# A two-convolution residual layer by lookup on one core: the first two blocks' patch sets as double sets of six transfers, with the transfer queue's order and one image's statistics moved

## The chip, the cores and the metric

The kernel runs on one of the eight cores of a Trainium2 chip. A core has TensorE (PE in the profile: the matrix array; PEld is its weight load), VectorE (DVE), ScalarE (ACT), GpSimd (POOL) and SyncE (SP, which in this kernel only starts transfers). Each engine takes its instructions in the order in which they were written and waits for others by semaphores. Transfers between the chip's main memory (DRAM) and the core's on-chip memory (SBUF) run on 16 DMA engines beside the compute engines; PE writes its results into PSUM banks, which other engines read out.

The metric is the device time of one execution in microseconds (us). Shown are the median of several executions and one execution taken by the profiler.

## The reference

Input `x` is 16 images of 256 channels of 28 x 28, float32. The layer is

```python
h   = gn(x)                        # group norm, 32 groups of 8 channels
out = relu(bn1(amm(h, centroids1, wsub1)))
out = bn2(amm(out, centroids2, wsub2))
out = out * sigmoid(relu(mean(out) @ w1 + b1) @ w2 + b2)     # per channel
y   = x + relu(out + h)
```

`amm` stands for a 3 x 3 convolution done approximately: for each channel the 9 values under the window (the patch, zero padded) are compared with 16 centroids of that channel, and the sum over all channels of a softmax-weighted lookup is the output:

```python
d    = sum(p * p) - 2 * p . centroid + sum(centroid * centroid)
attn = softmax(-d over the 16 centroids)
out  = sum over channels and centroids of attn * (centroid @ wsub)
```

The kernel uses that the sum over centroids of attn times centroid is a soft-selected patch of nine values per channel (numerators over a weight sum), which is then multiplied with `wsub` as an ordinary matrix product over 9 x 256 values.

## The kernel before, in words

**Tiling.** Two convolutions (l = 0, 1) times 16 images times four blocks make 128 blocks. A block is half of the channels (`hh`, 128 of 256) on half of the image rows (`t`, 14 of 28, N = 392 positions); the four blocks of an image go in the order (hh, t) = (0,0), (0,1), (1,1), (1,0). Images are numbered from 0, and so are blocks.

**One block.** (1) `patches` (L395) reads the nine shifted copies of the padded rows of 128 channels from a padded image in DRAM (`home1`, `home2`) into two SBUF tiles, p = 0 and 1, each of 8 slots with 8 channels per slot: six transfers per tile (the list `PIECES`), so twelve per block. A transfer writes every 8th partition (16 partitions) or, for three of the six, every 16th (8 partitions). One row of the tile per channel is a constant 1, written once at the start. (2) `logits` (L409) multiplies the patches with the centroids: four groups `mm` = 0 to 3 of 16 products; mm 0 and 1 read tile p = 0, mm 2 and 3 tile p = 1. Results `lg` lie in PSUM. (3) `exps` (L420, ACT) writes e = exp(2 lg), two instructions per group. (4) `num_b` (L474) forms the weight sums `nb` from the four e; ACT and DVE put them together (L484, L488, L494, L499), DVE takes the reciprocal (L502) and spreads it over partitions (`spread`, L517, two shuffles per group). (5) `num_a` (L460) forms the numerators `na` from e; three groups are read out by DVE with the reciprocal multiplied in (`scale_a`, L536), the others copied by ACT (`copy_a`, L530) and multiplied by POOL (`scale_q`, L525). The results are the tiles `qp` (pairs) and `qo`. (6) `product` (L544) multiplies nine such tiles with a weight matrix into `acc`. The products of the four blocks are combined as in a Strassen scheme of seven products, one of them issued in two parts: weights A11, A12, A22 and the sums S1 to S4, made by `combine` (L226), and differences of the q tiles, made by `mix` on POOL (L553).

**The start.** The weights and image 0 are loaded, `norm0` takes the group norm of image 0 for each channel half (`gn_stats` L339/L340 on DVE, the mean over groups by two small products on PE, L345 and L362, their read-outs on DVE, L349 to L364, the inverse root on POOL, L276 to L368, and `gn_apply` L374 on ACT into a padded tile `xpad`), and `to_home1` (L386) writes that tile to DRAM, where the patches come from. `center_wd` prepares the centroid weights.

**Where the tiles lie.** `pts` are the two ordinary patch tiles. Block 1 reads its patches into `alts`, which are the not yet filled weight tiles `walls` (two tiles of three weight matrices), so that it need not wait for block 0 to be done with `pts`. The twelve pair tiles `qp0` to `qp11` are separate tiles.

**Order.** There is no scheduler at work: `at(cl, sub, f, ...)` files every step under a key (clock, sub), and at the end all are issued in the order of the keys. So the key alone sets where a step stands on each engine's queue. A block takes two clocks. SP's order at the start is: the two halves of channel half 0 to `home1`; twelve patch transfers of block 0; channel half 1 to `home1` (key -0.95); twelve of block 1 (-0.9 and -0.4); six of block 2's first tile (0, 1.5); weight A11 (0, 1.55); image 1 (0, 1.65); six of block 2's second tile; weights S3 and A22; block 3; and so on. Issues that depend on a landing, or on a buffer's last reader, hold up everything behind them on SP.

**Statistics of the next image.** Image 1's `gn_stats` has key (3, 1.3), its two small products (4, 0.81) and (4, 0.83), in the midst of the first product, which is cut into three parts (0.8, 0.82, 0.84) of 4, 2 and 3 weight slices around them. Image 2's load has (6, 2.6) and its `gn_stats` (8, 0.3).

## Time and profile before

| what | value |
|---|---|
| median of 3 executions | 2630.59 us (2630.03 to 2636.79) |
| the profiled execution | 2632.19 us, of which the profile's span is 2630.7 us |
| PE busy | 2587.2 us, 98% of the span |
| VectorE, ScalarE, GpSimd busy | 1766.0, 1360.6, 1902.8 us (67%, 52%, 72%) |
| DMA | 374.37 MB in 217831 packets, mean 142 GB/s |

The profile is of one execution. Times in it are counted from the start of the span. A row of the timeline gives start, length, engine, line, operation, what it writes and reads, how many instructions are merged in it, and in brackets the engine's idle time before it with what ended that. [...] Rows of engine "SPq" are the issues of transfers: their length is the time of issuing, not of the transfer. In the chain of work that ended last a row "DMA a<-b" runs from a transfer's issue to its landing. "PEclk" is the share of TensorE's full clock that was granted.

### The profile page before, as it was taken

To read this page: it belongs to the slowest core of one execution; us is meant where nothing else is said; L and a number is where in the kernel's file an instruction comes from. 1 tells how busy PE (TensorE), PEld (TensorE's weight loads), DVE (VectorE), ACT (ScalarE), POOL (GpSimd) and SP (SyncE) were. 2 spreads that over 40 slices of the span, in tenths; PEclk is the share of its full clock that TensorE was granted. 3 is DMA by queue.
4 is the path that set the end of the run, shared out by engine and by line. 5 is a ranking of instruction groups with operands and counts; after the bars stand their busy time and mean duration, and the time that the engine had idled before them with its cause. 6 is when DMAs were issued, how large, how long until landed. Compare 5 with 4: busy or idle time off the path is not lost.

```text
span 2630.7 us, 85667 instructions
## 1 busy us (share of the span) xinstructions
PE 2587.2 (98%) x36984; PEld 1267.9 (48%) x36984; DVE 1766.0 (67%) x3759; ACT 1360.6 (52%) x1876; POOL 1902.8 (72%) x1320
## 2 busy tenths in 40 slices
PE   6999999999999999999999999999999999999997
PEld 2444454444544445444444444444444444444444
DVE  5776566666567665666666776767776667767665
ACT  4444444445444444444454555555555655555653
POOL 3876667766667766677667777778878787777786
PEclk9999999999999999999999999999999999999999
DMA  8656655665455566655664444444444444444441
GB/s 209 163 154 180 186 162 162 189 182 165 140 147 146 175 184 173 173 151 154 169 168 107 111 116 117 127 115 117 106 126 128 118 118 110 117 119 125 114 121 47
DMA packets 217831, 374.37 MB, mean 142 GB/s; under 512 B 29752, under 2 KB 188008, under 8 KB 217448
## 3 DMA queue, kind: packets, MB, share of 16 engines
q1 hardware_dynamic: 211272, 336.16, 47.8%
q0 software_dynamic: 6176, 32.66, 3.4%
q8 instruction: 295, 4.83, 0.8%
q14 instruction: 88, 0.72, 0.1%
HBM read 288.93 MB, written 79.80 MB: 140 GB/s over the span
## 4 chain that ended last, share of the span: by engine, by line
PE 96%; DMA 2%; DVE 1%; POOL 0%; ACT 0%; SPq 0%; issue 0%; DVEq 0%; POOLq 0%; ACTq 0%
PE acc L544 52%; PE lg L409 17%; PE na L460 14%; PE nb L474 13%; DMA xt<-in_x 1%; DMA wall<-home 1%; DMA pt<-home 0%; PE sep L846 0%; DVE gn_st L339 0%; DVE rb L517 0%; SPq L395 0%; DMA home<-xpad 0%; POOL qp L553 0%; PE sep L835 0%; PE gnp L362 0%
## 5 line engine op out<-in xcount | busy, mean ns | idle before, releaser
L544 PE MATMUL acc<-qp,wall 128*128 128x392 f32 x3072 | 1096.8, 500 | 1.7 <-POOL qp L553 0.9
L420 ACT ACTIVATE e<-lg 128x784 f32<-128x784 f32 x960 | 738.0, 821 | 638.2 <-PE lg L409 635.1
L553 POOL TENSOR_TENSOR qp<-qp,qp 128x784 f32<-128x784 f32 x512 | 944.9, 1869 | 158.6 <-DVE qp L536 158.1
L544 PEld LDWEIGHTS acc<-qp,wall 128*128 128x128 f32 x3072 | 565.2, 190 | 509.1 <-issue 55.3
L517 DVE STREAM_SHUFFLE rb<-r 128x392 f32<-128x392 f32 x1024 | 551.0, 605 | 0.0
L409 PE MATMUL lg<-pt,wd 32*32 32x392 f32 x16256 | 483.4, 502 | 7.3 <-DMA pt<-home 2.7
L488 DVE SCALAR_TENSOR_TENSOR r<-nb,kst,r 128x392 f32<-128x392 f32 x128 | 80.0, 625 | 452.6 <-ACT r L484 438.8
L536 DVE TENSOR_TENSOR qp<-na,rb 128x784 f32<-128x784 f32 x351 | 333.0, 972 | 64.7 <-PE na L460 53.7
L460 PE MATMUL na<-e,cwa 64*32 64x392 f32 x8192 | 374.8, 492 | 0.7 <-DVE hpad L581 0.7
L474 PE MATMUL nb<-e,cwb 64*32 64x392 f32 x8192 | 374.8, 493 | 0.1
L525 POOL TENSOR_TENSOR qo<-qo,rb 128x392 f32<-128x392 f32 x128 | 131.3, 1026 | 314.1 <-DVE rb L513 313.6
L502 DVE RECIPROCAL r<-r 128x392 f32<-128x392 f32 x128 | 333.2, 2603 | 4.4
L525 POOL TENSOR_TENSOR qp<-qp,rb 128x784 f32<-128x784 f32 x161 | 297.9, 1860 | 2.9
L474 PEld LDWEIGHTS nb<-e,cwb 64*32 64x32 f32 x8192 | 192.4, 107 | 174.3 <-issue 19.5
L460 PEld LDWEIGHTS na<-e,cwa 64*32 64x32 f32 x8192 | 182.9, 106 | 183.5 <-issue 76.2
L409 PEld LDWEIGHTS lg<-pt,wd 32*32 32x32 f32 x16256 | 121.2, 103 | 283.1 <-issue 252.1
L544 PE MATMUL acc<-qp,w_A 128*128 128x392 f32 x512 | 183.9, 502 | 0.0
L484 ACT ACTIVATE r<-nb,kst 128x392 f32<-128x392 f32 x128 | 86.7, 677 | 164.0 <-PE nb L474 164.0
L444 POOL TENSOR_TENSOR z<-z,mx 128x1568 f32<-128x1568 f32 x32 | 91.8, 2869 | 94.7 <-DVE mx L438 94.7
L544 PE MATMUL acc<-qo,wall 128*128 128x392 f32 x384 | 157.7, 492 | 0.0
L530 ACT COPY qp<-na 128x784 f32<-128x784 f32 x161 | 130.8, 812 | 27.0 <-PE na L460 25.2
L544 PEld LDWEIGHTS acc<-qp,w_A 128*128 128x128 f32 x512 | 95.0, 191 | 83.0 <-DVE qp L536 19.8
(154 smaller groups left out, 1646.8 us busy)
## 6 DMA issues: line engine op xcount, KB each, us to landing
pt<-home SPq DMA_DIRECT2D x762, 209.0 KB
pt<-home SPq DMA_DIRECT2D x762, 104.5 KB
home<-xpad SPq DMA_DIRECT2D x31, 899.0 KB
xt<-in_x SPq DMA_DIRECT2D x30, 784.0 KB
out_dram<-y SPq DMA_DIRECT2D x32, 392.0 KB
d_wS<-st SPq DMA_DIRECT2D x12, 192.0 KB
wall<-d_wS SPq DMA_DIRECT2D x4, 576.0 KB
wall<-in_ws SPq DMA_DIRECT2D x3, 576.0 KB
```

What stands on the lines that cost most here:

```text
L409: nc.tensor.matmul(bk[32 * c : 32 * c + 32, :N].rearrange("p (r w) -> p r w", w=W), lhsT=wts["wd", u["hh"]][32 * i : 32 * i + 32, mm, c, : ...
L420: nc.scalar.activation(eg[:, 2 * i : 2 * i + 2, :], bk[:, :, :N], AF.Exp, scale=2.0)
L444: nc.gpsimd.tensor_tensor(zk, zk, mx.unsqueeze(2).to_broadcast([P, N // 4, K]), ALU.subtract)
L460: nc.tensor.matmul(bs[32 * i : 32 * i + 32, r, :N], lhsT=wts["cwa", u["hh"]][64 * r : 64 * r + 64, mm, i, :], rhs=es[64 * r : 64 * r + 64, ...
L474: nc.tensor.matmul(bs[32 * i : 32 * i + 32, r, :N], lhsT=wts["cwb", u["hh"]][64 * r : 64 * r + 64, mm, i, :], rhs=es[64 * r : 64 * r + 64, ...
L502: nc.vector.reciprocal(u["r"], u["r"])
L517: nc.vector.stream_shuffle(rb[:, r, :], u["r"], mask_of(2 * mm + r))
L525: nc.gpsimd.tensor_tensor(q, q, u.pop(("rb", mm)), ALU.mult)
L530: nc.scalar.copy(pair(u, mm), u.pop(("na", mm))[:, :, :N])
L536: nc.vector.tensor_mul(pair(u, mm), u.pop(("na", mm))[:, :, :N], rb)
L544: nc.tensor.matmul(accs[key][:, :N], lhsT=wl[w][:, k, :], rhs=us["q", k], start=first and n == 0, stop=last and n == len(ks) - 1,)
L553: nc.gpsimd.tensor_tensor(pair(out_u, mm), pair(in0, mm), pair(in1, mm), ALU.subtract)
```

## The change

Blocks 0 and 1 get both of their patch tiles as one double set: six transfers of 16 slots instead of twelve of 8. Block 0's lies in the space of the pair tiles qp0 to qp8, which become one tile `qwall`; block 1's in the weights, which become one tile `wall`. Six setups of ones (four before) are filled at the start, POOL's two, ACT's four. On SP, channel half 1 goes to `home1` after block 1's set, and weight A11 ahead of block 2's first tile. Three of block 1's `spread` steps (six shuffles) move from before image 1's read-outs on DVE to between and behind them, and the first product is cut as 5, 2 and 2. Image 2's load goes behind block 4's second tile, and its `gn_stats` one clock later; image 1's channel half 1 goes to `home1` behind that load.

```diff
-    walls = [wpool.tile([P, 3, NS, P], F32, name=f"wall{i}") for i in range(NPT)]
-    wl = {n: walls[i // 3][:, i % 3] for i, n in enumerate(("S1", "S2", "S4", "A12", "S3", "A22"))}
+    wall = wpool.tile([P, 6, NS, P], F32, name="wall")
+    wl = {n: wall[:, i] for i, n in enumerate(("S1", "S2", "S4", "A12", "S3", "A22"))}
...
-    alts = [
-        w.rearrange("p a s n -> p (a s n)")[:, : 8 * PTW].rearrange("p (s n) -> p s n", n=PTW) for w in walls
-    ]
+    qwall = const.tile([P, 9, 2, N], F32, name="qwall")
+    both = [
+        t.rearrange("p a b n -> p (a b n)")[:, : 16 * PTW].rearrange("p (s n) -> p s n", n=PTW) for t in (qwall, wall)
+    ]
...
-        "pair": [const.tile([P, 2, N], F32, name=f"qp{i}") for i in range(NQ["pair"])],
+        "pair": [qwall[:, i] if i < 9 else const.tile([P, 2, N], F32, name=f"qp{i}") for i in range(NQ["pair"])],
...
+    def patches_both(u):
+        at0 = u["hh"] * P * 2 * HROW + RT * u["t"] * PW
+        n = PTW - 2
+        for dy, dx in PIECES:
+            step = 16 if dx else 8
+            o = both[u["r"]][TAPS[dy][dx] :: step, :, :n]
+            rows, slots = [step // 8 * HROW, P // step], [16 * HROW, 16]
+            nc.sync.dma_start(o, view(home1[0], at0 + dy * PW + dx, [rows, slots, [1, n]]))
...
-            u["pt", p] = alts[p] if j == 1 else pts[p]
-            if j == 1:
-                at(-0.4 if p else -0.9, 0.0, patches, u, p)
+            u["pt", p] = both[j][:, 8 * p : 8 * p + 8] if j < 2 else pts[p]
+            if j < 2:
+                if p == 0:
+                    at(*((-0.9, 0.0) if j else (-2, 1.5)), patches_both, u)
...
-                at(g - 1, 2.05 if i == 4 - len(kept) and j > 1 else 1.4 + 0.01 * i, spread, u, mm)
+                if j == 1:
+                    at(4, 0.835 if i else 0.815, spread, u, mm)
+                else:
+                    at(g - 1, 2.05 if i == 4 - len(kept) and j > 1 else 1.4 + 0.01 * i, spread, u, mm)
...
-                    for sub, k0, k1 in ((0.8, 0, 4), (0.82, 4, 6), (0.84, 6, 9)):
+                    for sub, k0, k1 in ((0.8, 0, 5), (0.82, 5, 7), (0.84, 7, 9)):
...
-                    at(*((g - 2, 2.6) if b else (0, 1.65)), load_x, b + 1)
+                    at(*((g - 2 + (b == 1), 2.6 - (b == 1)) if b else (0, 1.65)), load_x, b + 1)
...
-                        at(*((g, 0.3) if b else (3, 1.3)), gn_stats, b + 1, q)
+                        at(*((g + (b == 1), 0.3) if b else (3, 1.3)), gn_stats, b + 1, q)
...
-                        at(*((g + 4, 1.92) if b else (4 + 2 * q, 1.6)), to_home1, b + 1, q)
+                        at(*((g + 4, 1.92) if b else (4 + 3 * q, 1.6 + 0.05 * q)), to_home1, b + 1, q)
...
-    at(0, 1.55, load_w, 0, "A11")
+    at(0, 1.45, load_w, 0, "A11")
...
-    nc.scalar.activation(pts[0].rearrange("p s n -> p (s n)"), one.to_broadcast([P, 8 * PTW]), AF.Copy)
+    ones(both[0][:, :8], "act")
     norm0(0)
     for i in range(2):
         to_home1(0, 0, i)
-    nc.gpsimd.memset(pts[1], 1.0)
-    nc.gpsimd.memset(alts[0], 1.0)
-    nc.scalar.activation(alts[1].rearrange("p s n -> p (s n)"), one.to_broadcast([P, 8 * PTW]), AF.Copy)
+    ones(both[0][:, 8:], "pool")
+    ones(both[1][:, :8], "act")
+    ones(both[1][:, 8:], "pool")
+    for t in pts:
+        ones(t, "act")
...
-    at(-0.95, 0.7, to_home1, 0, 1)
+    at(-0.7, 0.7, to_home1, 0, 1)
```

`ones(t, eng)` fills a tile with 1.0, by an ACT activation or by a POOL memset.

More of the change, by code (lines that the diff above doesn't have):

```diff
@@ L1134, in center_wd, with ones @@
         center(wts["wd", hh].rearrange("p a b c -> p (a b c)"), 512)
-    nc.scalar.activation(pts[0].rearrange("p s n -> p (s n)"), one.to_broadcast([P, 8 * PTW]), AF.Copy)
+    def ones(t, eng):
+        t = t.rearrange("p s n -> p (s n)")
+        if eng == "act":
+            nc.scalar.activation(t, one.to_broadcast([P, 8 * PTW]), AF.Copy)
+        else:
+            nc.gpsimd.memset(t, 1.0)
+    ones(both[0][:, :8], "act")
     norm0(0)
```

## The prediction

> **What bounds the kernel now.** First the page: which engine is full, what the last chain consists of, and the size of the larger patch transfers.
>
> ```profile
> span 2630.7 us, 85667 instructions
> PE 2587.2 (98%) x36984; PEld 1267.9 (48%) x36984; DVE 1766.0 (67%) x3759; ACT 1360.6 (52%) x1876; POOL 1902.8 (72%) x1320
> PE 96%; DMA 2%; DVE 1%; POOL 0%; ACT 0%; SPq 0%; issue 0%; DVEq 0%; POOLq 0%; ACTq 0%
> ...
> pt<-home SPq DMA_DIRECT2D x762, 209.0 KB
> ```
>
> PE is the bound. It lacks 2630.7 - 2587.2 = 43.5 us, and all the change can touch is in there, or in slow records. Where it lies is told by the busy time by stretches (columns: stretch, its length, then busy us and instructions of PE, PEld, DVE, ACT, POOL, then granted clock, DMA share, GB/s).
>
> ```profile
> 0.00:20.00 20.00, 5.48 (x14) 3.51 (x14) 10.14 (x23) 8.22 (x4) 11.62 (x23) 1.00 0.74 217
> 40.00:60.00 20.00, 16.27 (x287) 6.61 (x271) 16.35 (x47) 10.54 (x15) 4.71 (x3) 1.00 0.98 216
> 120.00:140.00 20.00, 20.00 (x291) 10.02 (x290) 15.77 (x41) 10.32 (x15) 7.02 (x8) 1.00 0.32 82
> 2600.00:2631.00 31.00, 18.04 (x64) 10.28 (x62) 11.31 (x18) 11.49 (x21) 16.84 (x11) 0.83 0.14 55
> ```
>
> From 120 us on PE is full until the tail; 14.5 us are idle in the first stretch, 13.0 in the last, which isn't touched, and nearly all the rest between 20 and 120. So the change can win only what PE loses in there. PE's timeline shows the losses one by one:
>
> ```profile
> 23.64 3.21 PE L409 MATMUL lg<-pt,wd 32*32 32x392 f32 x64 [1.07 <-DVE wd L309]
> 29.07 2.63 PE L409 MATMUL lg<-pt,wd 32*32 32x392 f32 x64 [2.23 <-DMA pt<-home]
> 37.65 2.75 PE L409 MATMUL lg<-wall,wd 32*32 32x392 f32 x64 [2.30 <-DMA wall<-home]
> 49.25 2.07 PE L409 MATMUL lg<-pt,wd 32*32 32x392 f32 x48 [0.47 <-DMA pt<-home]
> 52.31 2.90 PE L544 MATMUL acc<-qp,w_A 128*128 128x392 f32 x8
> 56.47 0.39 PE L345 MATMUL gnp<-gn_mv,gmat 128*128 128x4 f32 x2 [1.26 <-DVE gn_mv L340]
> 59.95 0.38 PE L362 MATMUL gnp<-gn_dv,gmat 128*128 128x2 f32 x2 [1.67 <-DVE gn_dv L353]
> 61.11 2.82 PE L544 MATMUL acc<-qp,w_A 128*128 128x392 f32 x4
> 99.48 0.95 PE L409 MATMUL lg<-pt,wd 32*32 32x392 f32 x32 [1.99 <-DVE qo L499]
> 101.94 2.21 PE L460 MATMUL na<-e,cwa 64*32 64x392 f32 x48 [0.66 <-DVE hpad L581]
> ```
>
> Until 50 us PE waits for patches; around 56 to 60 for image 1's statistics; at 99.5 for DVE, which was late for another reason, shown below.
>
> **The change, part by part.** *The double sets.* Bytes and rows are the same; twelve issues become six. SP's issues, and the chain's transfers:
>
> ```profile
> 14.54 7.59 SPq L395 DMA_DIRECT2D pt<-home  x12
> 22.55 0.58 SPq L386 DMA_DIRECT2D home<-xpad  x1
> 23.40 12.08 SPq L395 DMA_DIRECT2D wall<-home  x12
> ```
>
> ```profile
> 10.37 4.15 DMA home<-xpad
> 19.66 6.55 DMA pt<-home
> 26.23 8.65 DMA wall<-home
> 34.89 7.98 DMA wall<-home
> 42.94 11.03 DMA xt<-in_x
> 54.00 1.05 DVE gn_st L339 x2
> 56.36 3.05 DVE rb L517 x6
> 80.36 12.99 DMA xt<-in_x
> ```
>
> Issues pause for landings (26.23 starts where the transfer of 19.66 lands, 34.89 where that of 26.23 does, 42.94 where that of 34.89 does), and the time to landing grows from 4 to 8 and 11 us: transfers queue up, and issuing (0.6 us each) is not the pace. What a single-tile set costs alone is seen where nothing else moves; the digits are the busy tenths of the DMA engines in 40 slices of 104 to 114 us, 0.25 us each:
>
> ```profile
> DMA  0000000200658965987989866444553100000000
> DMA packets 650, 0.99 MB, mean 99 GB/s; under 512 B 72, under 2 KB 648, under 8 KB 648
> ```
>
> 22 busy slices (the 11th to the 32nd), 5.5 us for 0.96 MB of patches: 11 us per block.
>
> Block 0: logits now start at 23.64 on half the set, and at 29.07 on the other half. All six long transfers span both tiles, so no logit can start before all land: between 23.64 and 29.07, near the upper end since the bytes are the same. I take 28.3: 0.8 less, because the write of channel half 1 (22.55) no longer mixes in. That is 4.7 us later than now for the first logits. What hid work there was ACT, whose exps of the first half ran before the second half was there; only the last four stand after it:
>
> ```profile
> 30.05 3.07 ACT L420 ACTIVATE e<-lg 128x784 f32<-128x784 f32 x4 [1.70 <-PE lg L409]
> 35.49 0.68 ACT L484 ACTIVATE r<-nb,kst 128x392 f32<-128x392 f32 x1 [2.37 <-PE nb L474]
> ```
>
> Afterwards all eight come in a row: 28.3 + 0.98 (30.05 - 29.07) + 2 x 3.07 + 2.37 = 37.8 for the sums' read-out, 2.3 late against 35.49. It costs only if block 1's patches aren't later still.
>
> Block 1: now its first tile is there at 37.65 and its second at 42.87 (34.89 + 7.98). Afterwards both together, 11 us of transfers after 28.3: 39.3. Bounds 37.65 and 42.87. So block 1's first logits start 39.3 - 37.65 = 1.65 later (0 to 5.2), and what hangs on them (its sums, then its reciprocal and image 1's statistics on DVE, then the first statistics product on PE) comes 1.65 later too: 56.47 + 1.65 = 58.1. Image 1's load (42.94 + 11.03 = 53.97) is just in time now.
>
> *The write of channel half 1* goes behind block 1's set, and block 2's first transfers read what it writes. It lands at 39.3 + at most 4.15, then 7.0 us for a set (104.0 plus 32 slices less its issue at about 105): 50.5. PE wants it at 49.25 - 0.47 + 1.65 = 50.4: no cost, but no slack. Behind that wait on SP stand image 1's load, block 2's second tile, S3 and A22, and go with it. The load's 0.8 MB take 4.6 us at a set's pace: 55.1, wanted at 54.00 + 1.65 = 55.65; what it is later than that counts in full. Weight A11, moved ahead of it, is used at 52.31; it costs nothing where it moves while SP waits for that write.
>
> *Six shuffles and the cut of the product.* The six (3.05 us at 56.36) stand before the read-out of the first product; that is the 1.67 wait at 59.95. Afterwards they stand behind. After 58.1: 0.39 for the product, then 0.54 for the read-outs on DVE (59.41 to 59.95), meanwhile PE does 4 records (2.90 / 8 each, 1.45): second product at 59.95, ending at 60.35, 4 more records, 61.8. In the trace `acc` ends at 61.11 + 2.82 = 63.93. Gain 2.1 us (3.75 if block 1 is not later, -1.45 at 5.2). Late next: two shuffles (0.51 each) stand before `gn_var` and four behind; the last ends at about 62.6, and the numerators that want them come at 61.8 + 0.95 (logits) + 0.74 (a third of 2.21) = 63.5.
>
> *Setups of ones.* ACT gets two more, before the second channel half's apply:
>
> ```profile
> 10.24 2.99 ACT L1142 ACTIVATE wall<-one 128x3360 f32<-128x3360 f32 x1
> 20.59 1.04 ACT L374 ACTIVATE xpad<-xt,nrm 128x784 f32<-128x784 f32 x1 [7.36 <-POOL nrm L368]
> ```
>
> 2 x 2.99 = 5.98 fit into the 7.36 us in which ACT waits for POOL: nothing; 1.4 us more and that write would be late, which goes last anyway. POOL's two stand where its two were.
>
> *Image 2.* Its load, issued at 80.36 amid others, lands at 93.35, and DVE, which stood 5.92 us idle for it, does 2.4 us of statistics (54.00 to 56.36 for image 1) before it turns to block 3's weight sums. That causes the 1.99 and 0.66 on PE:
>
> ```profile
> 93.37 1.04 DVE L339 BATCH_NORM_STATS2 gn_st<-xt 128x6 f32<-128x392 f32 x2 [5.92 <-DMA xt<-in_x]
> 102.81 2.72 DVE L536 TENSOR_TENSOR qp<-na,rb 128x784 f32<-128x784 f32 x3
> ```
>
> Together 2.65 lost. Afterwards the statistics stand between the last two shuffles and the three read-outs of `na`. From PE's end of product, t: DVE reads out `hpad` (0.5, as a shuffle of that size), shuffles 1.0, statistics 2.4, first read-out 0.9 (2.72 / 3): t + 4.8. PE's next logits, which want that bank, are ready after logits and numerators, 0.95 + 64/48 x 2.21: t + 3.9. So 0.9 us lost; I take 1.0 (0 to 2.4, all of the statistics). Gain 1.65 us (0.25 to 2.65). The load goes six issues (4 us) later and is wanted a clock later, some 10 us (2630.7 / 257): covered; at over 6 us more DVE would stand again as now. The write of image 1's channel half 1 behind it is read two clocks later: covered too.
>
> Sum: 2632.19 (the profiled execution, span 2630.7 and what lies around it) - 2.1 - 1.65 = 2628.4. The median shown, 2630.59, lies 1.6 under that execution, so 2626.8 for the median.
>
> **The rivals.**
>
> *Long transfers land sooner.* If issuing were the pace, six would save 3.8 us (half of 7.59) per block: block 0 at 29.07 - 3.8 = 25.3, its sums done at about 34, block 1 not waited for, 3.75 ahead of now instead of 1.65 behind. Then the first gain is 3.75 + 3.75 = 7.5, with 1.65 it makes 2630.59 - 9.15 = 2621.4: faster by 0.35%. Against it: growing times to landing, and a DMA share of 0.98 from 40 to 60 us. The Trainium skill's page "DMA: Bandwidth & Descriptors", section "Rules for kernel authors", says to join many small transfers into a large one, as small ones pay mostly overhead; that would bring this case about. The trace bears it out little: they are 209 KB or half of that here, and overlap.
>
> *Half-rate clock.* After a stretch in which PE waits, its clock is halved for a while:
>
> ```profile
> 30.00:32.00 2.00, 2.00 (x43) 0.59 (x46) 0.00 (x0) 1.95 (x3) 0.00 (x0) 0.51 0.76 210
> 32.00:34.00 2.00, 2.00 (x40) 0.70 (x32) 0.00 (x0) 1.12 (x2) 0.00 (x0) 0.64 0.66 165
> ...
> 62.00:64.00 2.00, 2.00 (x19) 0.58 (x34) 0.00 (x0) 0.00 (x0) 0.23 (x1) 0.50 0.51 160
> ```
>
> The first came after the 2.23 wait, the second after 1.26 and 1.67. The change makes PE's wait before the first logits longer and puts one of up to 2 us before block 1's. The first period took 2 x (0.49 + 0.36) = 1.7 us of PE. Two or three more of them, where PE and not ACT sets the pace (39 to 52 us), cost 3.4 to 5.1 and decide from 3.75 on: up to 2626.8 + 5.1 = 2631.9, slower. The Trainium skill's "TensorE: Matmul & The Clock Gate", section "HAM oscillation — how this bites in real kernels", speaks against the change here: idle gaps over about 3.4 us throttle PE to half rate. By that rule the gap before 28.3 costs a period, which falls where ACT is the pace; the rows agree that a gap is followed by a half-rate period, though gaps of 2.2 us were enough.
>
> *Block 2 late.* If A11 (0.59 MB, 0.6 of a set, 3.3 us) isn't hidden behind the wait for the write, block 2's first tile lands at 53.8 instead of 50.5, 3.4 us late, and the median is 2630.2: no difference.
>
> **How the numbers follow.** Forecast 2626.8 with its own range 2624.2 to 2631.8 (gains 6.4 to -1.2, both bounds together): 0.59. Sooner landing, around 2621: 0.17. Half-rate clock: 0.12. Block 2 late: 0.12. The range 2620 to 2633.5 holds 0.8. A measurement of this kernel tells about 0.3%, 7.9 us, from no change; only the sooner landing reaches that: faster 0.16, slower 0.07 (half-rate periods that go on, or a stall not seen here), within 0.77.
>
> **What would show it.** In the changed profile: first logits at about 28.3 waiting for a DMA into `qwall`, with no second wait; block 1's at about 39.3; statistics products at 58 and 60 with under 0.3 us before the second; no DVE wait for image 2, and about 1.1 us before logits in front of the product near 101; PE full from about 101. Wrong if the first logits start near 25 (sooner landing), the clock's tenths stay low between 39 and 52, or PE idles for a transfer near 50.

## The result and the profile after

The changed kernel takes 2636.96 us (median of 20 executions, 2632.54 to 2643.07); the kernel before, run beside it, 2631.22 us (2629.37 to 2636.79, 20 executions). The ratio is 1.002 with a 95% interval of 1.0013 to 1.0027: slower by 5.7 us, and 3.5 us past the end of the range that was given. The profiled executions stand 4.3 us apart (spans 2635.0 and 2630.7 us).

The page of the changed kernel, the engines' busy time:

```profile
PE 2587.3 (98%) x36984; PEld 1264.8 (48%) x36984; DVE 1766.5 (67%) x3759; ACT 1366.8 (52%) x1878; POOL 1902.5 (72%) x1320
```

PE has the same 2587 us of work as before; the 4.3 us are idle time or slow records. Busy time by stretches (same columns as in the prediction) tells where; first the kernel before, then the changed one:

```profile
20.00:40.00 20.00, 13.50 (x260) 4.65 (x258) 7.36 (x17) 9.78 (x13) 4.07 (x8) 0.91 0.87 200
```

```profile
20.00:40.00 20.00, 7.16 (x132) 3.09 (x130) 4.12 (x13) 4.77 (x7) 4.10 (x9) 1.00 1.01 185
40.00:60.00 20.00, 17.52 (x336) 5.77 (x329) 10.49 (x24) 12.01 (x18) 4.72 (x3) 0.83 0.75 184
```

Between 20 and 40 us PE works only 7.16 us, where before it worked 13.50; between 40 and 60 it is granted 0.83 of its clock, where before it had 1.00; from 120 to 140 us it works all 20.00, as before. PE's timeline (a product gives two records: the nine weight slices of a `product` are 18):

```profile
34.62 5.67 PE L419 MATMUL lg<-qwall,wd 32*32 32x392 f32 x128 [11.99 <-DMA wall<-home]
...
45.43 4.09 PE L419 MATMUL lg<-wall,wd 32*32 32x392 f32 x64 [2.31 <-DMA wall<-home]
...
56.38 2.86 PE L484 MATMUL nb<-e,cwb 64*32 64x392 f32 x64
...
66.64 0.38 PE L346 MATMUL gnp<-gn_mv,gmat 128*128 128x4 f32 x2 [0.24 <-DVE gn_mv L341]
...
68.28 0.28 PE L363 MATMUL gnp<-gn_dv,gmat 128*128 128x2 f32 x2
68.42 1.56 PE L554 MATMUL acc<-qwall,w_A 128*128 128x392 f32 x4
...
108.37 0.95 PE L419 MATMUL lg<-pt,wd 32*32 32x392 f32 x32 [1.12 <-DVE qwall L546]
109.35 2.87 PE L554 MATMUL acc<-qwall,wall 128*128 128x392 f32 x8
```

Against the rows of before:

| mark | before | after | later by |
|---|---|---|---|
| block 0's first logits | 23.64 | 34.62 | 10.98 |
| block 1's first logits | 37.65 | 45.43 | 7.78 |
| first statistics product | 56.47 | 66.64 | 10.17 |
| logits behind the first product | 63.86 | 69.92 | 6.06 |
| start of the product that stood at 105.01 | 105.01 | 109.35 | 4.34 |
| end of the span | 2630.7 | 2635.0 | 4.3 |

So block 1's logits lose 7.78 us, the way from there to the first statistics product another 2.4, then 4.1 are won back around the statistics products and 1.7 around image 2, as the change was expected to do (of the 4.1, some 1.5 are a half-rate clock in the profiled execution of before, see `m2_shuffles`). What failed is the patches. (The mark of 105.01 carries the span: in every kernel below the span stands 2524.8 to 2527.7 us behind it, so nearly all that tells them apart lies before it. One trace places a mark to about 2 us: block 1's first logits stand at 37.65, 37.65, 36.88 and 35.66 us in the kernel before and in the three below that leave the patches as they were.)

The chain of waits in the changed kernel, followed back from 70 us (start, length, what; a DMA row runs from issue to landing), and SP's issues:

```profile
11.11 5.17 DMA home<-xpad
...
27.41 17.88 DMA wall<-home
```

```profile
16.41 3.83 SPq L408 DMA_DIRECT2D qwall<-home  x6
20.34 7.67 SPq L408 DMA_DIRECT2D wall<-home  x6
...
34.33 0.34 SPq L213 DMA_DIRECT2D w_A<-in_ws  x1
```

Two things are new. The first patch transfer leaves at 16.41, not at 14.54: channel half 0 goes to `home1` in two parts of 64 channels, the first of which is there at 14.5 and the second at 11.11 + 5.17 = 16.28. A single tile's transfer reads 64 channels, hence only the first part; a transfer of 16 slots reads all 128. And the last transfer of block 0 lands at about 34.3 (weight A11, which waits for it on SP, leaves at 34.33), 17.9 us after the first issue, where before all twelve took from 14.54 to 29.07. The last transfer of block 1 (27.41) takes 17.88 us to land, and PE starts on block 1 when it is there.

### The profile page after: what moved, and what is told of

Its sections match the earlier page's. It is cut to its first block, busy times and chain, and to the rows that moved or that the text cites. A ratio compares the mean times of both kernels' runs of the same rounds, so it can differ in the third digit from the quotient of the medians.

```text
span 2635.0 us, 85658 instructions
## 1 busy us (share of the span) xinstructions
PE 2587.3 (98%) x36984; PEld 1264.8 (48%) x36984; DVE 1766.5 (67%) x3759; ACT 1366.8 (52%) x1878; POOL 1902.5 (72%) x1320
## 4 chain that ended last, share of the span: by engine, by line
PE 96%; DMA 1%; DVE 1%; ACT 0%; POOL 0%; SPq 0%; issue 0%; DVEq 0%; ACTq 0%; POOLq 0%
PE acc L554 52%; PE lg L419 17%; PE na L470 14%; PE nb L484 14%; DMA wall<-home 1%; DMA qwall<-home 0%; DVE cst L314 0%; DMA home<-xpad 0%; DVE r L512 0%; PE sep L856 0%; DVE rb L527 0%; DMA cwa<-in_cwa 0%; ACT e L430 0%; POOL qwall L563 0%; DVE gn_st L340 0%
## 5 line engine op out<-in xcount | busy, mean ns | idle before, releaser
L554 PE MATMUL acc<-qwall,wall 128*128 128x392 f32 x2304 | 827.6, 500 | 1.3 <-DVE qwall L546 0.7
L554 PEld LDWEIGHTS acc<-qwall,wall 128*128 128x128 f32 x2304 | 424.0, 190 | 381.3 <-issue 39.2
L563 POOL TENSOR_TENSOR qwall<-qwall 128x784 f32<-128x784 f32 x272 | 503.7, 1870 | 78.9 <-DVE qwall L546 78.5
L546 DVE TENSOR_TENSOR qwall<-na,rb 128x784 f32<-128x784 f32 x283 | 268.8, 972 | 50.5 <-PE na L470 40.2
L554 PE MATMUL acc<-qp,wall 128*128 128x392 f32 x768 | 279.5, 500 | 0.0
L535 POOL TENSOR_TENSOR qwall<-qwall,rb 128x784 f32<-128x784 f32 x133 | 245.9, 1859 | 2.5
L563 POOL TENSOR_TENSOR qwall<-qp,qwall 128x784 f32<-128x784 f32 x96 | 178.4, 1875 | 77.6 <-DVE qp L546 77.6
L554 PEld LDWEIGHTS acc<-qp,wall 128*128 128x128 f32 x768 | 141.3, 190 | 127.1 <-issue 14.7
L563 POOL TENSOR_TENSOR qp<-qwall,qp 128x784 f32<-128x784 f32 x96 | 178.1, 1869 | 0.1
```

The lines of the kernel that those rows point to most:

```text
L535: nc.gpsimd.tensor_tensor(q, q, u.pop(("rb", mm)), ALU.mult)
L546: nc.vector.tensor_mul(pair(u, mm), u.pop(("na", mm))[:, :, :N], rb)
L554: nc.tensor.matmul(accs[key][:, :N], lhsT=wl[w][:, k, :], rhs=us["q", k], start=first and n == 0, stop=last and n == len(ks) - 1,)
L563: nc.gpsimd.tensor_tensor(pair(out_u, mm), pair(in0, mm), pair(in1, mm), ALU.subtract)
```

## The experiments

Two accounts of the late patches were set against each other first: LONG, the transfers of 16 slots land late by themselves, and MIX, block 1's set, now straight behind block 0's with no write between, takes the DMA engines from it. Times in the text below are of profiled executions; ratios are against the kernel before, run beside on the same chip. The experiments ran on three chips, on which the kernel before has medians of 2632.78 us (`s1` to `s4`), 2631.43 (`s5`, `c1`, `m2`, `m3`) and 2631.88 (`c2`, `c3`, `m1`, `m4`), so kernels are compared here by their distance to it.

**Both blocks in twelve transfers again** (`s1_singles`).

```diff
-                if p == 0:
-                    at(*((-0.9, 0.0) if j else (-2, 1.5)), patches_both, u)
+                at(*((-0.4 if p else -0.9, 0.0) if j else (p - 2, 1.5)), patches, u, p)
```

> The changed kernel, but the patches of blocks 0 and 1 again come in twelve transfers of 8 slots each, into the same double tiles and in the same order on SP (channel half 1's write still behind block 1's set). Theory LONG (the 16-slot transfers are what lands late: each needs both parts of channel half 0 before it starts, and a set is whole only at the end): first logits back near 23.6 us and the second half of block 0 near 29, block 1's first half at 35 to 38; the gains of the moved shuffles (4.1) and of image 2 (1.7) stay, so the median is 2624 to 2627. Theory MIX (block 1's set, now straight behind block 0's with no write between, takes DMA engines from it, whatever the size): the second half of block 0 still comes at 32 to 35, block 1's at 40 to 45, and the median is 2628 to 2635.

Measured: 2637.1 us, ratio 1.0015 (1.0006 to 1.0024). Neither: the first six transfers left at 14.69 as before, yet PE's timeline has

```profile
30.02 5.89 PE L419 MATMUL lg<-qwall,wd 32*32 32x392 f32 x128 [7.35 <-DMA qwall<-home]
43.71 4.25 PE L419 MATMUL lg<-wall,wd 32*32 32x392 f32 x64 [5.00 <-DMA w_A<-in_ws]
```

All 128 logits of block 0 stand in one row at 30.02. In the kernel before the same six transfers were no limit for a start at 23.64 (that start waited for DVE). So the first half's logits waited for the second half's transfers. (The second row names A11's load as what ended the wait, by inference; block 1's logits read `wall` and the centroids.) That asked for a further experiment.

**The same, with a tile per half** (`s5_two_tiles`).

```diff
-    wall = wpool.tile([P, 6, NS, P], F32, name="wall")
...
+    walls = [wpool.tile([P, 3, NS, P], F32, name=f"wall{i}") for i in range(NPT)]
...
-    qwall = const.tile([P, 9, 2, N], F32, name="qwall")
+    qwalls = [const.tile([P, 5, 2, N], F32, name=f"qwall{i}") for i in range(NPT)]
...
-            u["pt", p] = both[j][:, 8 * p : 8 * p + 8] if j < 2 else pts[p]
+            u["pt", p] = both[j][p] if j < 2 else pts[p]
...
```

> As s1_singles, but the space of the numerators and that of the weights are two tiles each, one per half of a block, instead of one tile that both halves share. Theory TILE (in s1_singles block 0's first logits waited for the second half's transfers only because both halves lie in one tile): first logits at 23.6 us again, second half at 30, block 1's first half at 35 to 38 and its second without or with a short wait, end of the first product near 63 or before, median 2626 to 2630. Rival QUEUE (the wait comes from the order of the transfers on SP, with channel half 1's write behind block 1's set): logits again in one stretch at 30, block 1's at 43 to 44, median 2636 to 2638.

Measured: 2629.5 us, ratio 0.9989 (0.998 to 0.9998).

```profile
23.73 3.30 PE L420 MATMUL lg<-qwall,wd 32*32 32x392 f32 x64 [1.10 <-DVE wd L311]
30.23 3.30 PE L420 MATMUL lg<-qwall,wd 32*32 32x392 f32 x64 [3.21 <-DMA qwall<-home]
...
37.62 1.81 PE L420 MATMUL lg<-wall,wd 32*32 32x392 f32 x48
```

TILE holds, QUEUE falls: with the order of the transfers unchanged, the logits start per half again, and block 1's at 37.62 without any wait. Where two halves are slices of one tile, this program waits for the writes of both. (The first product ends at 64.34 us, not at 63 or before as expected; PE's clock is halved here from 47 to 53 us, see the runs on the clock.) The same twelve transfers come out 4.3 us over the kernel before in one tile per block and 1.9 us under it with a tile per half. The edit also parts the weights and the numerators into two tiles each, but the two traces are 6.1 us apart at block 1's first logits already, and 5.6 at the mark of 105.01.

Two more things follow. The new order on SP, with the write behind block 1's set, does not by itself make block 1's logits late: `s5_two_tiles` has it too. And joining two transfers to one is hardly it either: `s1_singles` has twelve and is 4.3 us over before (1.6 to 6.3), the changed kernel with six 5.7 (3.4 to 7.1). What costs is that the logits wait for a block's whole set.

**Only block 0 in twelve transfers** (`s2_b0_single`; its two halves still in one tile).

```diff
-                if p == 0:
-                    at(*((-0.9, 0.0) if j else (-2, 1.5)), patches_both, u)
+                if j == 0:
+                    at(p - 2, 1.5, patches, u, p)
+                elif p == 0:
+                    at(-0.9, 0.0, patches_both, u)
```

> The changed kernel with only block 0's set back to twelve transfers of 8 slots; block 1's stays a set of six. Theory LONG: block 0's logits at 23.6 and near 29, block 1's at 40 to 43 (one wait instead of two halves), median 2626 to 2631. Theory MIX: block 0's second half at 32 to 35, block 1's near 45, median 2632 to 2636.

Measured: 2634.32 us, ratio 1.0005 (0.9996 to 1.0014).

```profile
30.63 5.97 PE L419 MATMUL lg<-qwall,wd 32*32 32x392 f32 x128 [7.98 <-DMA qwall<-home]
42.32 3.81 PE L419 MATMUL lg<-wall,wd 32*32 32x392 f32 x64 [2.92 <-DMA wall<-home]
```

Block 0 is at 30.63 for the reason just found, which neither account had. Block 1's logits are at 42.32 as LONG had it. This is the set of block 1 with the write moved behind it and block 0's twelve ahead: it lands hardly earlier than the second half did in the kernel before (42.87). The write's move brought it next to nothing.

**The write between the sets again** (`s3_home_between`).

```diff
-    at(-0.7, 0.7, to_home1, 0, 1)
+    at(-0.95, 0.7, to_home1, 0, 1)
```

> The changed kernel with channel half 1's write back between the two sets (before block 1's set). Theory MIX: block 0's logits start at 28 to 30 instead of 34.6, block 1's at 42 to 44, median 2631 to 2634. Theory LONG: block 0's logits still start at 33 to 35, block 1's are pushed by the write to 48 to 50, median 2638 to 2642.

Measured: 2638.85 us, ratio 1.0024 (1.0014 to 1.0034).

```profile
31.77 5.83 PE L419 MATMUL lg<-qwall,wd 32*32 32x392 f32 x128 [9.17 <-DMA wall<-home]
46.39 4.30 PE L419 MATMUL lg<-wall,wd 32*32 32x392 f32 x64 [6.00 <-DMA wall<-home]
```

Between the two: block 0 comes 2.9 us sooner than in the changed kernel (so what stands behind it does matter, for MIX), block 1 comes 1.0 later, and the median is LONG's.

**Block 1's set held until block 0's has landed** (`s4_hold`).

```diff
+    held = const.tile([P, 1], F32, name="held")
+
+    def hold():
+        nc.sync.dma_start(held, both[0][:, 0, 0:1])
+
+    at(-0.95, 0.7, hold)
     at(-0.7, 0.7, to_home1, 0, 1)
```

> The changed kernel with a small transfer on SP between the two sets that reads block 0's patches, so that block 1's set is issued only when block 0's has landed whole. It measures what a set of six takes alone. Theory MIX: block 0's set lands in 11 us after its first issue at 16.4, logits at 27 to 29; block 1's at 40 to 43; median 2630 to 2634. Theory LONG: block 0's set takes 16 to 18 us even alone, logits at 33 to 35, block 1's at 50 to 54, median 2640 to 2646.

Measured: 2639.78 us, ratio 1.0027 (1.0017 to 1.0037). SP and PE:

```profile
16.35 3.82 SPq L408 DMA_DIRECT2D qwall<-home  x6
30.06 0.55 SPq L1172 DMA_DIRECT2D held<-qwall  x1
```

```profile
30.30 5.67 PE L419 MATMUL lg<-qwall,wd 32*32 32x392 f32 x128 [7.71 <-DMA qwall<-home]
45.84 4.22 PE L419 MATMUL lg<-wall,wd 32*32 32x392 f32 x64 [7.03 <-DMA wall<-home]
```

Alone, block 0's set takes 30.06 - 16.35 = 13.7 us, and its logits start at 30.30 instead of 34.62. So of the 6.3 us by which the prediction's 28.3 was exceeded, 1.9 are the later first issue and 4.3 are block 1's set running beside; both accounts named a part, and neither has block 1's 45.84. Where the neighbour's price is paid is seen in the busy time by stretches (the last two columns are the share of the 16 DMA engines and GB/s), first of the changed kernel, then of this one:

```profile
21.00:25.00 4.00, 1.22 (x2) 0.50 (x2) 2.58 (x6) 0.69 (x1) 3.41 (x5) 1.00 1.07 227
26.00:29.00 3.00, 0.00 (x0) 0.00 (x0) 0.24 (x2) 0.00 (x0) 0.00 (x0) 1.00 1.10 115
```

```profile
21.00:25.00 4.00, 1.22 (x2) 0.50 (x2) 2.58 (x5) 0.66 (x1) 3.40 (x5) 1.00 0.95 204
25.00:28.00 3.00, 0.00 (x0) 0.00 (x0) 1.10 (x8) 0.00 (x0) 0.00 (x0) 1.00 0.53 123
```

Towards its end a set uses only half of the DMA engines (its transfers of 8 partitions are left): alone, from 25 to 28 us, the share is 0.53 and the rate 123 GB/s. In the changed kernel block 1's first transfers fill the other half, all engines are busy (1.10), and yet they move 115 GB/s together, half of the 227 before. Block 0's last two transfers share that rate with block 1's. For block 1 the run-ahead gave back what it took: held, its logits come at 45.84, beside 45.43.

**The moves without the sets** (`c1_moves`: the kernel before with the shuffles, the cut and image 2's moves).

```diff
-                at(g - 1, 2.05 if i == 4 - len(kept) and j > 1 else 1.4 + 0.01 * i, spread, u, mm)
+                if j == 1:
+                    at(4, 0.835 if i else 0.815, spread, u, mm)
+                else:
+                    at(g - 1, 2.05 if i == 4 - len(kept) and j > 1 else 1.4 + 0.01 * i, spread, u, mm)
...
-                    for sub, k0, k1 in ((0.8, 0, 4), (0.82, 4, 6), (0.84, 6, 9)):
+                    for sub, k0, k1 in ((0.8, 0, 5), (0.82, 5, 7), (0.84, 7, 9)):
...
-                    at(*((g - 2, 2.6) if b else (0, 1.65)), load_x, b + 1)
+                    at(*((g - 2 + (b == 1), 2.6 - (b == 1)) if b else (0, 1.65)), load_x, b + 1)
...
-                        at(*((g, 0.3) if b else (3, 1.3)), gn_stats, b + 1, q)
+                        at(*((g + (b == 1), 0.3) if b else (3, 1.3)), gn_stats, b + 1, q)
...
-                        at(*((g + 4, 1.92) if b else (4 + 2 * q, 1.6)), to_home1, b + 1, q)
+                        at(*((g + 4, 1.92) if b else (4 + 3 * q, 1.6 + 0.05 * q)), to_home1, b + 1, q)
```

> The kernel before with only the moved shuffles, the new cut of the first product and the moves of image 2's load, statistics and write; patches, their space and SP's order at the start as before. Theory MOVES (these parts bring their gains by themselves, whatever the patches do): logits at 23.6, 29.1 and 37.7 as before, no wait before the second statistics product, end of the first product near 60.2 instead of 63.9, about 1 us lost before the logits in front of the next product instead of 2.65, median 5.4 under before (2.2 at the least). Rival COVER (the gains in the changed kernel came only because its patches were late and the engines behind had time): the shuffles or image 2's statistics delay something else, median within 1.5 of before.

Measured: 2628.09 us, ratio 0.9986 (0.9976 to 0.9995): faster than both kernels, by 3.3 us against before.

```profile
37.65 2.75 PE L409 MATMUL lg<-wall,wd 32*32 32x392 f32 x64 [1.43 <-DMA wall<-home]
...
56.35 0.39 PE L345 MATMUL gnp<-gn_mv,gmat 128*128 128x4 f32 x2 [0.31 <-DVE gn_mv L340]
...
58.00 0.28 PE L362 MATMUL gnp<-gn_dv,gmat 128*128 128x2 f32 x2
58.14 1.56 PE L544 MATMUL acc<-qp,w_A 128*128 128x392 f32 x4
...
97.96 0.95 PE L409 MATMUL lg<-pt,wd 32*32 32x392 f32 x32 [1.12 <-DVE qp L536]
98.93 4.19 PE L544 MATMUL acc<-qp,wall 128*128 128x392 f32 x12
```

MOVES holds, COVER falls: with block 1's logits at 37.65 as before, the first product ends at 59.7 instead of 63.93, and the product of 105.01 starts at 98.93. The trace wins 6.1 us there, some 1.5 of them by the clock (next run); the median, 3.3, with an interval of 1.3 to 6.3 us, is what repetitions give.

**The shuffles and the cut alone** (`m2_shuffles`, the first two hunks of the diff above).

> The kernel before with only the moved shuffles and the new cut of the first product. Theory MOVES: second statistics product without a wait, end of the first product near 60.2 instead of 63.9, the stall for image 2 near 97 still 2.65, median 3.75 under before (0.5 to 4). Rival COVER: a new wait of 2 us or more for the shuffles in front of the next numerators, median within 1 of before.

Measured: 2628.63 us, ratio 0.999 (0.9981 to 0.9999). PE's timeline of this kernel, and then of `m1_image2` below, which keeps the shuffles and the cut of before:

```profile
54.96 0.39 PE L345 MATMUL gnp<-gn_mv,gmat 128*128 128x4 f32 x2
...
56.74 1.56 PE L544 MATMUL acc<-qp,w_A 128*128 128x392 f32 x4
```

```profile
56.18 0.39 PE L345 MATMUL gnp<-gn_mv,gmat 128*128 128x4 f32 x2 [0.97 <-DVE gn_mv L340]
...
60.65 1.48 PE L544 MATMUL acc<-qp,w_A 128*128 128x392 f32 x4
```

From the first statistics product to the end of the first product it takes 54.96 to 58.30, 3.3 us, against 7.46 before: 4.1 less, and MOVES holds. But not all of the 4.1 is the moves'. In the profiled execution of before the last four records of that product took 2.82 us (61.11), at a clock granted at 0.50 from 62 to 64 us; here four take 1.56. `m1_image2`, with the same order as before and no half rate there, takes 56.18 to 62.13, 5.95 us. So the shuffles and the cut bring 2.6 us, and some 1.5 are the clock of that one execution. The median, 2.8 under before, agrees.

**Image 2 alone** (`m1_image2`, the last three hunks).

> The kernel before with only the moves of image 2's load and statistics and of image 1's second write. Theory MOVES: no wait of DVE for image 2's load near 93, some 1 us lost before the logits in front of the product that stands at 101 in before instead of 2.65 around it, median 1.65 under before (0.25 to 2.65). Rival COVER: another wait takes its place, median within 0.5 of before or over it.

Measured: 2631.05 us, ratio 0.9993 (0.9984 to 1.0002): 0.8 under before, by the time not to be told from it. The trace shows the stall as expected,

```profile
100.89 0.95 PE L409 MATMUL lg<-pt,wd 32*32 32x392 f32 x32 [1.12 <-DVE qp L536]
```

1.12 us in place of 1.99 and 0.66. From the end of the first product to the start of the product of 105.01 it is 39.7 us, 1.35 less than before; in the changed kernel and in `c1_moves` it is 1.7 and 1.85 less.

**One long set at a time, on top of the moves.** `c2_b0_double` gives `c1_moves` block 0's long set, in the space of the numerators, and `c3_b1_double` block 1's, in the weights; the write stays between.

```diff
...
+            if j == 0:
...
+                    at(-2, 1.5, patches_both, u)
+            elif j == 1:
+                at(-0.4 if p else -0.9, 0.0, patches, u, p)
...
```

```diff
...
+            if j == 1:
...
+                    at(-0.9, 0.0, patches_both, u)
...
```

> The kernel before with the moved shuffles, cut and image 2 (as c1_moves), and block 0's set as six transfers of 16 slots in the space of the numerators; block 1's stays twelve of 8 slots in two tiles, and channel half 1's write stays between them. Theory LONG: block 0's logits start near 31.8 (first issue at 16.4 and some 15 us to the last landing, with the write mixed in), all in one stretch; block 1's first half follows at 40 to 42 instead of 37.7; median 2.5 to 5 over c1_moves. Rival HARMLESS (block 0's lateness is covered, since only block 1's patches set the end): block 1's first half within 1 us of 37.7, median within 1 of c1_moves.

> As c1_moves, and only block 1's set as six transfers of 16 slots in one tile of the weights; block 0 as before. Theory LONG: block 0 at 23.6 and 29 as before, block 1's logits only when all six have landed, at 43 to 45 instead of 37.7; the first product ends 5 to 7 us later than in c1_moves, median 2633 to 2635.5. Rival SPREAD (with one long set the wait between 37.7 and 43 is filled by block 0's numerators, whose products come before block 1's second half anyway): first product 2 us later or less, median 2628 to 2630.

Measured: 2632.13 us (ratio 0.9999, 0.999 to 1.0008) and 2635.79 us (1.0014, 1.0005 to 1.0023), 0.3 and 3.9 us over the kernel before, where `c1_moves` is 3.3 under it: block 0's long set costs 3.6 us, block 1's 7.3. First block 0's, then block 1's:

```profile
32.62 5.67 PE L422 MATMUL lg<-qwall,wd 32*32 32x392 f32 x128 [9.97 <-DMA qwall<-home]
...
41.05 1.81 PE L422 MATMUL lg<-wall,wd 32*32 32x392 f32 x48
```

```profile
43.76 4.32 PE L418 MATMUL lg<-wall,wd 32*32 32x392 f32 x64 [7.36 <-DMA wall<-home]
```

LONG holds twice, HARMLESS and SPREAD fall: block 1's first logits are at 41.05 and at 43.76, not near 37.65. But with block 1's long set the first product ends at 70.12 us, 10.4 later than in `c1_moves` (59.70), not 5 to 7: 6.1 at the first logits, and most of the rest while PE's clock is halved (14.5 us from there to the end of the weight sums, against 11.3). Block 1's set is the dearer: its first half used to feed PE from 37.65 on, and now PE stands idle for 7.36 us until all six are there. Block 0's long set costs about what the moves bring, block 1's about twice that.

**The clock.** In the changed kernel the granted clock is halved between 45 and 52 us. Two kernels fill one of PE's two waits with needless products: `m3_warm` the 2.31 us before block 1's logits, `m4_warm_first` the 12 us before block 0's.

```diff
+        warm = 24 if u["w"] == 1 and mm == 0 else 0
...
+            for k in range(warm):
+                c = k % 4
+                nc.tensor.matmul(
+                    bk[32 * c : 32 * c + 32, :N].rearrange("p (r w) -> p r w", w=W),
+                    lhsT=wts["wd", u["hh"]][0:32, mm, c, :],
+                    rhs=both[0][0:32, c, :].rearrange("p (r w) -> p r w", w=PW)[:, :, :W],
...
```

```diff
+        warm = 15 if u["w"] == 0 and mm == 0 else 0
+        flat = wts["wd", u["hh"]].rearrange("p a b c -> p (a b c)")
...
+            for k in range(warm):
+                nc.tensor.matmul(bk[:, :N], lhsT=flat[:, :P], rhs=flat[:, :N], start=True, stop=True)
```

> The changed kernel with 24 needless products on PE in front of block 1's first logits (from block 0's patches, overwritten by the true ones), which fill the wait for block 1's patches. Theory CLOCK (that wait halves PE's clock and so costs some 2.7 us between 45 and 57): the granted clock stays near 1.0 from 45 to 52, block 1's weight sums end 11 to 11.5 us after its first logits instead of 13.8, median 2634 to 2635.5. Rival HIDDEN (the half clock costs nothing, another engine sets the pace there, or it only moves to another place): median within 1 of the changed kernel, 2636 to 2638.

> The changed kernel with 15 needless full-array products on PE in front of block 0's first logits, which fill most of the wait of 12 us before 34.6 (they go to a bank that the true logits overwrite). Theory CLOCK (the half rate from 45 to 52 is the answer to that long wait): the granted clock stays 1.0 from 45 to 57, block 1's weight sums end 11 to 11.5 us after its first logits instead of 13.8, median 1.5 to 2.7 under the changed kernel. Rival DENSITY (the half rate answers the thin work between 34 and 57, small products with waits, whatever came before): half rate again between 42 and 57, median within 1 of the changed kernel.

Measured: 2637.83 us (ratio 1.0025, 1.0014 to 1.0036) and 2636.57 us (1.0014, 1.0005 to 1.0023). Busy time by stretches, the third column from the end is the granted clock; the changed kernel, `m3_warm`, `m4_warm_first`:

```profile
45.00:48.00 3.00, 2.57 (x54) 1.00 (x56) 3.00 (x4) 0.92 (x2) 0.00 (x0) 0.56 0.49 193
```

```profile
42.00:45.00 3.00, 3.00 (x44) 1.14 (x40) 1.41 (x4) 1.25 (x2) 0.00 (x0) 1.00 0.55 167
45.00:48.00 3.00, 3.00 (x49) 1.55 (x42) 2.96 (x5) 0.00 (x0) 0.00 (x0) 0.60 0.40 145
```

```profile
45.00:48.00 3.00, 2.06 (x56) 0.91 (x64) 3.00 (x4) 1.13 (x2) 0.00 (x0) 1.00 0.52 202
```

With the short wait filled (PE busy 3.00 of 3.00 ahead of 45 us) the clock is halved all the same; CLOCK falls for that wait. With the long wait filled it stays at 1.00, as CLOCK had it and DENSITY had not, with the same thin work between 36 and 57 us. The median goes the other way: within 1 us of the changed kernel, as DENSITY had it, and not 1.5 to 2.7 under it.

Two other traces speak against the long wait as the whole cause, with a fixed delay. In `c2_b0_double` PE waits 9.97 us before block 0's logits, and its half rate comes from 50.2 to 53.6 us only, 17.6 us after that wait; in the changed kernel it comes 10.7 us after it, and in `m3_warm` 12.1, all of which PE works without a gap. And `s5_two_tiles`, which between 23 and 46 us has no wait over 3.21, is halved all the same:

```profile
47.00:53.00 6.00, 6.00 (x80) 1.54 (x64) 2.56 (x9) 1.58 (x2) 4.69 (x3) 0.50 1.01 189
```

So a filled long wait took the half rate away in one execution, and what sets it off stays open.

The column has a limit, too: early in a trace it reads 1.00 where PE is at half rate. The mean length of PE's records shows it (behind the bar: busy us, mean ns; then the idle time before). The changed kernel from 34.6 to 38.4 us, where the column reads 1.00, from 45.5 to 52 (0.50) and from 52.2 to 59 (1.00); then `c1_moves` from 23.5 to 27 (1.00):

```profile
L419 PE MATMUL lg<-qwall,wd 32*32 32x392 f32 x86 | 4.3, 835 | 12.0 <-DMA wall<-home 12.0
...
L419 PE MATMUL lg<-wall,wd 32*32 32x392 f32 x64 | 4.1, 855 | 2.3 <-DMA wall<-home 2.3
...
L419 PE MATMUL lg<-wall,wd 32*32 32x392 f32 x64 | 2.7, 499 | 0.2 <-ACT qwall L540 0.2
```

```profile
L409 PE MATMUL lg<-pt,wd 32*32 32x392 f32 x64 | 3.3, 854 | 1.0 <-DVE wd L309 1.0
```

The same products take 855 ns at half rate and 499 at full, so block 0's logits run at half rate, in the changed kernel as in `c1_moves`, and likewise in the kernel before (845 ns from 23.5 to 27 us). That early stretch is common to all; what the changed kernel adds is the one from 45 to 52 us. Its price is the way from block 1's first logits to the end of its weight sums: 45.43 to 56.38 + 2.86 = 59.24, 13.8 us, in the changed kernel; 45.88 to 57.0, 11.1 us, in `m4_warm_first`. The median shows little of these 2.7 us (5.7 over before became 4.7, with overlapping intervals), and neither does the trace in the end: 2.2 us ahead at the first statistics product, it is 0.8 ahead at the mark of 105.01, as PE now outruns a patch transfer:

```profile
91.65 0.95 PE L424 MATMUL lg<-pt,wd 32*32 32x392 f32 x32 [1.49 <-DMA pt<-home]
```

## Why the prediction was wrong

**The step that failed** is "I take 28.3: 0.8 less, because the write of channel half 1 (22.55) no longer mixes in", with its bounds 23.64 and 29.07, and with it "39.3", which hangs on it. Measured were 34.62 and 45.43, so block 1's first logits came 7.78 us later, where 1.65 (0 to 5.2) was forecast. Three things were mis-sized or missing.

- *The first issue.* The sum kept 14.54. A transfer that spans 128 channels also reads the second part of channel half 0, so it waits until 16.28 on SP: 1.9 us. The upper bound 29.07 was thus too low from the start. The dependence stood in the code (`to_home1` in two parts, `patches` of 64 channels).
- *The pace.* That "the bytes are the same" held for a set alone: 28.3 + 1.9 = 30.2, and `s4_hold` has 30.30. It did not hold beside block 1's set, which the moved write let come straight behind: 4.3 us more.
- *Block 1.* The distance of 11.0 between the two blocks' logits came out at 10.8, but by chance: it is 15.5 in `s4_hold`, where block 1's set starts when block 0's has landed, 13.7 in `s1_singles` and 11.7 in `s2_b0_single`. The 11 us of a lone set, read in another stretch of the trace, were taken as the pace of two sets, with the write's 4.15 us simply gone from in front. `s2_b0_single` shows block 1's set at 42.32 even with block 0's transfers short, hardly earlier than the last landing before (42.87). That row, taken as the bound, was the better estimate; with block 0's set long even it was passed by 2.6 us.

The two halves of block 1 were counted as first 37.65, second 42.87, afterwards both at 39.3, a loss of 1.65. Waiting for the last of six takes the whole way to the later landing, 5.2 us, unless the set itself becomes faster, and it didn't; `c3_b1_double`, with 43.76 for 37.65, shows that on its own.

**Steps that held.** PE is the bound and only the stretch before 120 us counts: the span stands 2525.65 us behind the mark of 105.01 in the changed kernel, 2525.7 before. The shuffles and the cut: no wait before the second statistics product, and the last shuffles delay nothing. That the traces have 4.1 us for the 3.75 forecast is luck in part: forecast and trace both start from the 63.93 of one execution whose clock was halved there, and `m2_shuffles` against `m1_image2` gives 2.6. Image 2: 1.0 lost, 1.65 won by the forecast, 1.12 and 1.72 by the trace. The ones on ACT and POOL cost nothing seen. The move of channel half 1's write, A11 and what stands behind cost nothing at block 2, whose logits start without a wait for a DMA; that is a smaller merit, as block 1 was so late that there was slack.

**The rivals.** Sooner landing is refuted: the sets land later, and `c2_b0_double` and `c3_b1_double` lose 3.6 and 7.3 us against `c1_moves`, each measured from the kernel before on its chip. The rule of the Trainium skill that was named with it ("DMA: Bandwidth & Descriptors", section "Rules for kernel authors") gives 64 KB as the size under which a transfer is mostly overhead; the transfers here had 209 KB or half of that already, and the runs show no gain from joining them. Block 2 late didn't occur. Half-rate clock, given 0.12, occurred, at 2.7 us and in the place where PE sets the pace. The prediction's reading that the half rate before from 30 us on followed a wait of 2.23 us isn't the whole: the products ahead of that wait ran at half rate already (845 ns). The Trainium skill's page "TensorE: Matmul & The Clock Gate", section "HAM oscillation — how this bites in real kernels", has gaps over about 3.4 us followed by half rate. The trace agrees as far as block 0's logits go, which run at half rate right behind the wait of 11.99 us, "where ACT is the pace", as the prediction said; but `c1_moves` has the same behind a wait of 0.97 us, its last gap over 3.4 us (5.69 us) having ended at 17.05. The stretch that cost time began 10.7 us after the wait, and no run here shows that it followed from it.

Together: 7.78 later at block 1's logits, 2.39 more to the statistics products (the half rate), less 4.11, less 1.72: 4.34, and the span has 4.3. The forecast had 1.65 and nothing, less 3.75, less 1.65, and came out 3.75 under before. (The terms are of two executions; some 1.5 of the 4.11 are the clock in that of before.)

## What to carry to other kernels

A transfer that is joined from two takes over the waits of both (1.9 us here) and hands over at the later of both (43.76 for 37.65): before counting issues saved, list what the parts were waiting for and who was already working on the first one. Two halves that are to be used one after the other want a tile each; as slices of one tile they were waited for together here, even with a transfer each. And when one change holds several edits, measure each alone: here the two good ones (3.3 us) were buried under a bad one (5.7 + 3.3 = 9 us). A gain read from two single traces can also hold a clock that was halved in one of them: compare the lengths of like records before it is counted.

## What was not expected of the hardware

All 16 DMA engines busy is no measure of the rate: at 1.07 busy they moved 227 GB/s, and at 1.10 they moved 115 with two sets' transfers on different halves of the engines, no more than half of the engines alone (0.53, 123). What the packets then wait for no run here shows; it stays open.

The granted clock in the profile is no measure of PE's rate early in a trace: it reads 1.00 while the same products take 835 to 855 ns that take 499 at full rate. Later it agrees with their length (855 ns at 0.50). A half rate can come during full work: in the changed kernel from 45.4 to 52.2 us, 10.7 us after a wait of 11.99; in `c2_b0_double` 17.6 us after one of 9.97; in `s5_two_tiles` from 46.5 us with no wait over 3.21 since 23 us. Filling the wait of 12 us with full-array products removed it in one execution, filling the one of 2.31 with small products did not. What sets it off stays open.
